# Layer 1 of a graph network on one core: the sums of s and t move from ScalarE to VectorE, with s in a PSUM bank

## The chip, the core and the metric

The kernel runs on one core of a Trainium2 chip: TensorE (PE in the profile; PEld is its weight load), VectorE (DVE), ScalarE (ACT), GpSimd (POOL) and SyncE (SP), which work side by side and wait for each other by semaphores. SBUF is the working memory; PSUM, 8 banks of 128 partitions x 512 fp32, is where TensorE writes. The metric is the time of one execution on the device in microseconds (us); less is better. Before the change the median of nine runs is 1860.69 us (1857.22 to 1868.44).

## What is computed

Two layers over 4096 nodes of 512 features, with one sparse 4096 x 4096 adjacency matrix, all in fp32. Layer 0 is a graph convolution. Layer 1, in which the change lies, is an attention layer. The reference, cut to it:

```
h = relu(layernorm(x))
s = (h @ W) @ a[:512]            # one number for each destination node i
t = (h @ W) @ a[512:]            # one number for each source node j
e = leaky_relu(s[i] + t[j], 0.2)
attention = softmax(where(adj > 0, e, -1e12), axis=1)
negative  = -softmax(where(adj > 0, -e, -1e12), axis=1)
x = x + elu(concat([attention @ h, negative @ h]) @ wtrans)
```

## The kernel before

**Layer 0** (the first 950 us or so) multiplies the dense adjacency and x, builds lists of neighbours, and writes to HBM eight tables with one row for each node: its 512 features, its t, and mask bytes. These tables are filled in part by copies from one to the next; the last ones (`copy_rows`, L498) are issued by SyncE while layer 1 runs.

**Layer 1** (`sparse_layer1`) goes through 62 blocks of 64 destination nodes, two to a pair; a pair is a tile of 128 nodes. (Two more blocks, those of `PAIR0` = 16, are done ahead of it.) The pairs come in the order 17, 20, 18, 19, 21, 22 and so on; k counts the blocks in that order from 0, so even k is the first block of a pair and odd k its second. Row r is the block's number (pair 19 has the blocks 38 and 39).

For each pair, GpSimd gathers rows of a table by index (`gather1`, L506) into three tiles g of 8, 7 and 7 chunks of 128 neighbours. One of the 22 chunks is the pair's own 128 rows, which SyncE loads plainly (`load_own`, L520) as the last chunk of the middle tile. The first block of a pair uses the first two tiles, its second block the last two; each block so has two parts, and the middle tile is the second part of the first block.

`weights(r)` makes the weights of a block, part by part. A part has n chunks (7 or 8) and 64 columns for each:

- z = s + t for each chunk: ScalarE, one instruction for each chunk (L1765), 128x64, with t as its bias. s is a row of the block's s, broadcast over the partitions, in SBUF.
- y = 0.2 z (ScalarE, L1767), z = max(z, y) (VectorE, L1768), e = exp(z) and z = exp(-z) (ScalarE, L1773).
- p = mask > 0 times e, and the same with z (VectorE, L1777, two for each part).

z and e are PSUM banks. After both parts, one reduction on VectorE (L1787, "total") adds the block's weights over its chunks.

`product(r)` has TensorE sum "total" over the partitions (cs, L580), multiply the weights and the gathered rows into u (L556, 40 or 44 matmuls of 128x512), and VectorE invert the sums (rl, L585 and L588); ScalarE scales u into us (L1815). `turn` transposes us (tp, L595; ScalarE copies it out, L602). `project1` multiplies by `wtrans` (o, L1826): its first half at odd k, its second in `finish1` at the next even k. `finish1` then takes the minimum with 0 (eo, L1843), exp (L1844), the maximum plus x1 (y, L1846) and the last sum (eo, L1847), and SyncE stores the tile (L1848). The load of x1 for a tile (L1838) and the store stand in SyncE's queue ahead of the next table copies and own load.

For each k the program is written in the order `product(r_k)`; table copies when k % 6 is 1; `gather1` two pairs ahead; `weights` of the block two places ahead; `turn` of the block before; the half of a projection. A scheduler sets each engine's own order from that; GpSimd's gathers and a few others are pinned to the written order. Every PSUM tile (z, e, cs, u, tp, o) is one bank from a pool of eight, handed out in the written order, and as the built program shows the bank chosen is the one whose last reader comes earliest. The first instruction that writes a bank waits for the last reader of the tile that held it before.

`RB` is 64, a block's columns; `ROW_T` is the column of t in a table row. `scores` (L524) is an older helper by which VectorE sums s and t of a whole part in one instruction; before the change only the blocks done ahead of the 62 use it, with s in SBUF.

## Time and profile before

One execution was profiled; it took 1864.22 us, of which the span of the instructions is 1862.4.

| what | value |
|---|---|
| median of nine runs | 1860.69 us |
| profiled execution, and its span | 1864.22 us, 1862.4 us |
| busy in the span: PE, DVE, ACT, POOL | 1835.8, 1274.3, 936.2, 826.0 us |
| L1765, ScalarE's sums by chunk | 899 instructions (s, s_first), about 320 ns each |
| L1768, L1777, VectorE, 128x448 or 128x512 | 0.62 to 0.70 us each |
| L1787, VectorE's reduction | 62, 3373 ns each |
| L506, GpSimd's gathers | 672, 956 ns each |
| 1200 to 1300 us: PE, DVE, ACT, POOL busy | 100.0, 55.9, 60.6, 75.0 us |
| 1500 to 1600 us: PE, DVE, ACT, POOL busy | 100.0, 67.2, 70.8, 75.4 us |

How to read the views: a line of groups or of a timeline names a source line, engine, operation, the tile written and those read (buffer numbers left out), and its time. "[1.94 <-DVE rl L585]" at its end is the idle time of that engine just before it, and whose event ended it by the profile; where several were waited for, the last is named, and an engine's event may be a neighbour of the one that mattered. Times of a timeline count from the start of the span. A lower TensorE clock shows as longer matmuls.

### The profile page before, as it was taken

How to read it: one execution, taken by the hardware profiler on the slowest of the kernel's cores; microseconds unless marked ns; L12 is line 12 of the kernel's file. 1: busy time of each engine (PE TensorE's matmuls, PEld its weight loads, DVE VectorE, ACT ScalarE, POOL GpSimd, SP SyncE). 2: the span in 40 equal slices, each digit the busy share in tenths (PEclk: the TensorE clock that was granted, in tenths of full speed). 3: DMA queues.
4: the chain of work that ended last, by engine and by line, in shares of the span. 5: the costliest groups of instructions: out<-in, count | busy, mean ns of one | idle time of the engine just before them, and what ended most of it. 6: DMA issues, size and time to landing. Idle time of an engine off the chain costs nothing.

```text
span 1862.4 us, 24509 instructions
## 1 busy us (share of the span) xinstructions
PE 1835.8 (99%) x7708; PEld 1040.0 (56%) x7708; DVE 1274.3 (68%) x2758; ACT 936.2 (50%) x2165; POOL 826.0 (44%) x919
## 2 busy tenths in 40 slices
PE   8999999999999999999999999999999999999998
PEld 3444448888888888888644333333333333333333
DVE  6766669798979998897344566565656567665661
ACT  6777763322222321222235576665766677666661
POOL 3101000012332122422167677777776777777740
PEclk9999999999999999999998999999999999999999
DMA  9999976849685859585899789999898999989860
GB/s 370 402 333 333 336 236 201 250 154 297 196 254 162 281 159 291 155 268 155 251 324 362 250 271 320 339 303 333 287 340 275 335 298 297 299 281 300 298 213 25
DMA packets 217219, 504.33 MB, mean 271 GB/s; under 512 B 35060, under 2 KB 69396, under 8 KB 217079
## 3 DMA queue, kind: packets, MB, share of 16 engines
q0 software_dynamic: 62560, 233.71, 37.9%
q1 hardware_dynamic: 114240, 236.49, 37.7%
q10 hardware_dynamic: 40278, 32.47, 5.7%
q8 instruction: 63, 1.03, 0.2%
q14 instruction: 78, 0.63, 0.1%
HBM read 457.77 MB, written 103.45 MB: 301 GB/s over the span
## 4 chain that ended last, share of the span: by engine, by line
PE 85%; DMA 6%; DVE 3%; ACT 3%; issue 2%; POOL 1%; ACTq 0%; DVEq 0%; SPq 0%
PE p L1105 33%; PE u L556 24%; PE o L1826 10%; PE acc L1064 5%; PE yp L890 5%; DMA g<-table 3%; PE q L1465 3%; DMA ar<-in_adj 2%; PE tp L595 1%; ACT z L1765 1%; DMA g<-table,idx 1%; PE counts L867 1%; POOL g L506 1%; PE tx L831 1%; PE cs L1541 1%
## 5 line engine op out<-in xcount | busy, mean ns | idle before, releaser
L506 POOL DMA_INDIRECT g<-table,idx x672 | 642.6, 956 | 290.3 <-issue 171.3
L556 PE MATMUL u<-g,p 128*64 128x512 f32 x2604 | 574.2, 596 | 0.0
L556 PEld LDWEIGHTS u<-g,p 128*64 128x64 f32 x2604 | 183.1, 137 | 339.2 <-issue 313.7
L442 POOL DMA_INDIRECT ld<-lst,off x160 | 144.3, 902 | 344.4 <-DMA ld<-lst,off 165.8
L1765 ACT ACTIVATE z<-s,g 128x64 f32<-128x64 f32 x812 | 259.8, 320 | 52.6 <-DMA g<-table 30.3
L1105 PE MATMUL p<-y,at 128*128 128x256 f32 x832 | 248.0, 380 | 0.0
L1105 PE MATMUL p<-y,sums 128*128 128x256 f32 x832 | 247.4, 379 | 0.0
L1105 PE MATMUL p<-t,sums 128*128 128x256 f32 x832 | 245.3, 379 | 0.0
L1826 PE MATMUL o<-wt,ut 128*128 128x512 f32 x496 | 228.1, 604 | 8.6 <-DVE rl L585 7.2
L1768 DVE TENSOR_TENSOR z<-z,y 128x512 f32<-128x512 f32 (+1 forms) x124 | 80.5, 649 | 213.8 <-ACT y L1767 211.4
L1787 DVE TENSOR_REDUCE total<-p 128x128 f32<-128x1920 f32 (+1 forms) x62 | 209.1, 3373 | 2.1
L1105 PEld LDWEIGHTS p<-t,sums 128*128 128x128 f32 x832 | 158.0, 190 | 21.7 <-issue 0.2
L1105 PEld LDWEIGHTS p<-y,at 128*128 128x128 f32 x832 | 157.1, 190 | 23.2 <-issue 2.2
L1105 PEld LDWEIGHTS p<-y,sums 128*128 128x128 f32 x832 | 158.0, 190 | 21.5
L1826 PEld LDWEIGHTS o<-wt,ut 128*128 128x128 f32 x496 | 91.1, 194 | 102.1 <-issue 92.0
L930 ACT ACTIVATE m<-at 128x1024 uint8<-128x1024 f32 x110 | 113.1, 1047 | 54.1 <-DVE prod L1020 15.3
L852 ACT ACTIVATE junk<-ar 128x1024 bf16<-128x1024 f32 x128 | 134.5, 1051 | 9.3 <-DMA ar<-in_adj 5.2
L1777 DVE SCALAR_TENSOR_TENSOR p<-g,e 128x512 f32<-128x512 uint8 (+1 forms) x124 | 79.1, 638 | 74.4 <-ACT e L1773 51.6
L1105 PE MATMUL p<-t,at 128*128 128x256 f32 x416 | 124.0, 380 | 1.2 <-DVE w L975 1.2
L1064 PE MATMUL acc<-y,at 128*128 128x512 f32 x256 | 120.2, 594 | 0.0
L890 PE MATMUL yp<-w_sb,hx_t 128*128 128x512 f32 x256 | 118.5, 606 | 0.4 <-DVE hx_t L836 0.4
L800 ACT ACTIVATE rrb<-rrb 128x1 f32<-128x1 f32 x32 | 6.5, 203 | 214.1 <-DVE rrb L799 209.8
(220 smaller groups left out, 2038.0 us busy)
## 6 DMA issues: line engine op xcount, KB each, us to landing
ar<-in_adj SPq DMA_DIRECT2D x128, 512.0 KB, 6.2
at<-in_adj_t SPq DMA_DIRECT2D x112, 512.0 KB, 5.3
table<-table SPq DMA_DIRECT2D x49, 1032.0 KB, 9.3
table<-m ACTq DMA_DIRECT2D x48, 256.0 KB, 8.0
g<-table,idx POOLq DMA_INDIRECT x672, 5.0
g<-table SPq DMA_DIRECT2D x32, 322.0 KB, 6.0
at<-in_adj_t SPq DMA_DIRECT2D x32, 256.0 KB, 7.0
xr<-in_x SPq DMA_DIRECT2D x32, 256.0 KB, 6.2
```

Of the source, the lines that this page charges most:

```text
L442: return nc.gpsimd.indirect_dma_start(out=lst_dram[g][e % TURNS][:, :], out_offset=bass.IndirectOffsetOnAxis(ap=off[g][:, e, c : c + 1], a ...
L506: i = nc.gpsimd.indirect_dma_start(out=gt[:, k, :], out_offset=None, in_=table[2 * n // RPT], in_offset=bass.IndirectOffsetOnAxis(ap=idx[n ...
L556: i = nc.tensor.matmul(u[h * RB : (h + 1) * RB], p[:, k, h].rearrange("p g i -> p (g i)"), row(k), start=begin and k == HALVES[r % 2][h][0 ...
L852: nc.scalar.activation(junk, ar, AF.Identity, accum_out=parts[j][:, c : c + 1])
L890: nc.tensor.matmul(yp, hx_t[j][:, c * P : (c + 1) * P], w0_sb[:, c, :], start=c == 0, stop=c == FC - 1,)
L930: nc.scalar.activation(m, at, AF.Sign)
L1064: nc.tensor.matmul(a, at[:, 0, it * P : (it + 1) * P], y0[j], start=j == 0, stop=j == NJ - 1)
L1105: i = nc.tensor.matmul(out, left[:, x * P : (x + 1) * P], right, start=jp == 0 and first, stop=jp == NP - 1 and (final or not first),)
L1765: nc.scalar.activation(z[:, c], s, AF.Identity, bias=t[:, c])
L1768: nc.vector.tensor_tensor(z, z, y, ALU.max)
L1787: nc.vector.tensor_reduce(total, q, AX.X, ALU.add)
L1826: i = nc.tensor.matmul(halves[j], uts[j][:, g, c, :], wts[g][:, c, :], start=g == 0 and c == 0, stop=g == 1 and c == FC - 1,)
```

## The change

- The pool of eight PSUM banks can be replaced in mid-program: `new_banks` closes it and opens others. After the step k = 6 it opens one bank of its own, "row", and a pool of seven for everything else.
- From then on (the blocks from the tenth of the order on, since `weights` runs two places ahead), ScalarE copies the row of s for four pairs (128x512) into that bank when a new row begins, seven times in all.
- `weights` then calls `scores` once for each part, with s read from that bank, in place of ScalarE's instruction for each chunk.
- The pools of PSUM wait by tile (`reuse_waits="tile"`), as those of SBUF did already.

```diff
-    ps = ctx.enter_context(tc.tile_pool(name="ps", bufs=8, space=PSUM))
+    psum = ctx.enter_context(ExitStack())
+    ps = {}
+
+    def new_banks(name, n, own=()):
+        psum.close()
+        for tag in (*own, "ps"):
+            bufs = n if tag == "ps" else 1
+            pool = tc.tile_pool(name=f"{name}{tag}", bufs=bufs, space=PSUM, reuse_waits="tile")
+            ps[tag] = psum.enter_context(pool)
+
+    new_banks("all", 8)
...
-                s = srow[r // 8][:, r % 8 * RB : (r % 8 + 1) * RB]
+                s = srow[r // 8]
+                if "row" in ps:
+                    if r // 8 not in s_bank:
+                        s_bank.clear()
+                        s_bank[r // 8] = ps["row"].tile(
+                            [P, 4 * P], F32, tag="row", name=f"s_bank{r // 8}"
+                        )
+                        nc.scalar.copy(s_bank[r // 8], s)
+                    s = s_bank[r // 8]
+                s = s[:, r % 8 * RB : (r % 8 + 1) * RB]
...
-                    for c in range(n):
-                        nc.scalar.activation(z[:, c], s, AF.Identity, bias=t[:, c])
+                    if "row" in ps:
+                        scores(s, z, t)
+                    else:
+                        for c in range(n):
+                            nc.scalar.activation(z[:, c], s, AF.Identity, bias=t[:, c])
...
+                if k == 6:
+                    new_banks("few", 7, ("row",))
```

The helper that is called, unchanged:

```
    def scores(s, z, t):
        n = z.shape[1]
        return nc.vector.tensor_tensor(
            z, t.to_broadcast([P, n, RB]), s.unsqueeze(1).to_broadcast([P, n, RB]), ALU.add
        )
```

More of the change, by code (lines that the diff above doesn't have):

```diff
@@ L328, in gcn_gat_kernel @@
     const = ctx.enter_context(sbuf(name="const", bufs=1))
-    ps = ctx.enter_context(tc.tile_pool(name="ps", bufs=8, space=PSUM))
+    psum = ctx.enter_context(ExitStack())
[7 more added lines that the diff above has]
+    new_banks("all", 8)
     dram = ctx.enter_context(tc.tile_pool(name="dram", bufs=1, space=DRAM))
     def bank(name):
-        return ps.tile([P, 512], F32, tag="ps", name=name)
+        return ps["ps"].tile([P, 512], F32, tag="ps", name=name)
     ones = const.tile([P, P], F32, name="ones")
@@ L591, in turn_u @@
     def turn_u(r, u, ut, pin=False):
-        tp = ps.tile([P, FC, 2, 2, SB], F32, tag="ps", name=f"tp{r}")
+        tp = ps["ps"].tile([P, FC, 2, 2, SB], F32, tag="ps", name=f"tp{r}")
         for c in range(FC):
@@ L712, in sum_counts @@
         def sum_counts(g):
-            o_ps = places[g] = ps.tile([NH, NE + 1, NK + 1], F32, tag="ps", name=f"o_ps{g}")
+            o_ps = places[g] = ps["ps"].tile([NH, NE + 1, NK + 1], F32, tag="ps", name=f"o_ps{g}")
             for e in range(NE + 1):
@@ L1878, in sparse_layer1 @@
             with_late = (2 * pairs[0], 2 * pairs[0] + 1)
-            lates, halves = {}, {}
+            lates, halves, s_bank = {}, {}, {}
             order = [r for n in pairs for r in (2 * n, 2 * n + 1)]
```

## The prediction

> **What bounds the kernel now.** I first read the page's busy shares: TensorE is busy for 99% of the span, at nearly full clock. Busy only says where to look, so the next view is the chain that ended last, and the third is what TensorE waited for in layer 1 (from 950 us on).

> ```profile
> PE 1835.8 (99%) x7708; PEld 1040.0 (56%) x7708; DVE 1274.3 (68%) x2758; ACT 936.2 (50%) x2165; POOL 826.0 (44%) x919
> PEclk9999999999999999999998999999999999999999
> PE 85%; DMA 6%; DVE 3%; ACT 3%; issue 2%; POOL 1%; ACTq 0%; DVEq 0%; SPq 0%
> ```

> ```profile
> PE o L1826 <- DVE rl L585: 7.2, 4, 2.6
> PE o L1826 <- DVE y L1846: 1.3, 1, 1.3
> PE o L1860 <- ACT ut L602: 0.5, 1, 0.5
> ```

> The second fence (us in total, times, longest) is the point: after 950 us TensorE stands still for 9.0 us in all. A pair of blocks costs it 26.6 us (44 products 9.6, turn and projection 4.1, sums 0.2, 40 products 8.7, the same again), end to end. So ScalarE work that goes away is worth nothing in itself; only those gaps can shrink, and the gap that a new wait makes is paid in full.

> Where are the gaps? The TensorE timeline shows them at 1026.3 (2.6 us) and 1058.9 (1.35), both before the first block that the change touches, then at 1300.9 (1.94), 1382.9 (2.2) and 1466.8 (0.46). The last three have one cause, here for 1300.9 (timelines of SyncE, ScalarE, VectorE, TensorE; start, us, instruction, idle before it):

> ```profile
> 1271.17 2.54 SPq L498 DMA_DIRECT2D table<-table  x3
> 1274.02 0.68 SPq L520 DMA_DIRECT2D g<-table  x1
> ...
> 1294.16 0.32 ACT L1765 ACTIVATE z<-s,g 128x64 f32<-128x64 f32 x1 [7.83 <-DMA g<-table]
> ...
> 1301.98 0.68 DVE L1846 SCALAR_TENSOR_TENSOR y<-o,x 128x512 f32<-128x512 f32 x1
> ...
> 1302.81 3.67 PE L1826 MATMUL o<-wt,ut 128*128 128x512 f32 x8 [1.94 <-DVE rl L585]
> ```

> Every sixth step (k = 13, 19, 25, 31) SyncE puts three table copies ahead of the load of the block's own rows; that load lands 22.5 to 23.0 us after the first copy is issued (an own load without copies ahead lands in 6.0). ScalarE's sum of that one chunk waits, VectorE's total and y come 8.4 us after the landing, and the next projection waits for y to free its bank. k = 13 passes: there y ends at 1220.07 and the projection starts at 1220.91. The 2.2 us gap also costs clock: the eight projections after it took 5.37 us, not 3.60.

> **The change, part by part.**

> 1) ScalarE. Blocks from the tenth of the order on (53 of 62) lose their chunk sums: 768 of the 899 of L1765, at 320 ns, are 246 us, and 7 copies into the bank (nearest row: 128x512 in 0.60) add 4. All of it lies beside TensorE: 0 us by itself. Between copies, totals come every 24.9 us when VectorE and ScalarE catch up (1298.0, 1322.9, 1347.8), so the weights' chain regains only 1.7 us per pair; with 9.3 us less ScalarE in a pair it becomes bound by the gathers instead.

> 2) VectorE gains 106 sums of a part. The trace shows none from PSUM. Nearest rows: L527, the same sum from SBUF, 621 and 693 ns; L1768, which reads and writes PSUM, 633 and 699. I take 0.65, ends 0.62 and 0.75; VectorE was 60% busy in this stage and gets 2.6 us more in 26.6, hidden. [...]

> 3) GpSimd must not be slowed: its 21 gathers of a pair at 0.95 us plus 0.30 issue take 26.3 of 26.6 us. L1768 and L1777 run among them with one operand in SBUF, and the gathers beside them stay at 0.95. The new sum has that form: 0.

> 4) Banks: 8 become 7 after k = 6. In the changed kernel as built, TensorE's order is unchanged but its waits are not. At k = 7 the sum of block 39 (cs) takes the bank of the projection o of node tile 20 and waits for that tile's y. Before, it took the bank of the sum before it. TensorE's and VectorE's rows there:

> ```profile
> 1100.12 3.60 PE L1826 MATMUL o<-wt,ut 128*128 128x512 f32 x8
> 1103.56 0.28 PE L580 MATMUL cs<-ones,total 128*128 128x1 f32 x2
> 1103.76 9.66 PE L556 MATMUL u<-g,p 128*64 128x512 f32 x44
> ```

> ```profile
> 1107.25 3.51 DVE L1787 TENSOR_REDUCE total<-p 128x128 f32<-128x1920 f32 x1
> 1110.67 0.68 DVE L1843 TENSOR_SCALAR eo<-o 128x512 f32<-128x512 f32 x1
> 1111.27 0.68 DVE L1846 SCALAR_TENSOR_TENSOR y<-o,x 128x512 f32<-128x512 f32 x1
> ```

> TensorE is ready at 1103.56; y ends at 1111.95, behind a 3.5 us reduction, and VectorE's order up to it is unchanged. All products and projections stand behind that cs: **+8.4 us**, once (ends 7 and 9.5, as ScalarE's chain in front of the reduction shifts). Then the clock: after the 2.6 us gap at 1026.3 eight projections took 6.56 us (3.0 lost), after 2.2 us 1.8 were lost, after 1.94 none. For 8.4 us I take **+2.5** (ends 0 and 3.4). [...]

> 5) The order on VectorE. In a pair's first block the sum of the second part now stands ahead of the two products p of the first part, and that sum waits for the own load. Before, those products ran while ScalarE waited. With 7 banks the sum and product of the block that TensorE is at wait for the banks which these two free. Price at k = 19, in the times of before: projection o ends at 1263.8, so y can end about 1265.5 (it was 1269.97, held back by ScalarE); rl, max and eo 1.4, issue 0.4: copies at 1267.3, own rows at 1290.0 (+22.7); sum 0.65, two products 1.25, 0.1 of signalling: 1292.0. TensorE wants the sum at 1290.42 and the product at 1290.62: **1.4 us**, at four places = 5.6. In return the old waits end: the y that caused them now comes 10.4 us after the landing, 1300.4, while the turn that needs it comes at 1300.2 + 1.4. So 1.94 + 2.2 + 1.8 of clock + 0.46 = **-6.4** go. Ends for the new waits: 0 (y so early that the rows land in time) and 2.7 us each with 1.8 of clock (y 1.2 later): 0 to 18.

> 6) SyncE: one 0.5 MB table copy moves ahead by a pair, and four loads of s ahead of an own load (0.8 us of issue; the own load lands 5 us before the gathers beside it: 1570.01 + 6.0 against 1576.6 + 4.8): 0, to +1.

> **Sum:** 8.4 + 2.5 + 5.6 - 6.4 + 1 (the chance of clock loss at the four places) = +11.1; I take **+11.5**. The profiled execution took 1864.22 us (span 1862.4 and 1.8 around it): 1875.7 by its own time. It stands 3.5 us above the median of the nine runs, 1860.69, and a median is wanted: **1872 us**.

> **The rivals.**

> A, faster. The bank wait at k = 7 is covered, because y of tile 20 comes before 1103.6, and the relieved ScalarE removes the three late gaps: -6.4 and new waits of at most 2, so 1856. For it: the gaps are ScalarE's and the copies' work. Against: y would have to come 8.4 us sooner, and nothing ahead of it on VectorE or ScalarE changes. It decides only if the wait costs under 2 us. 0.06.

> B, no change: the wait at k = 7 is half hidden (5 us with clock) and the four late places gain it back: 1861. 0.08.

> C, slower still: y comes 1 us later in the pairs before the copies, each of the four waits is 2.5 us, above the 2.2 that cost clock: 10.9 + 17 - 6.4 = +21.5, 1882. For it: 1.4 against 2.2 is a small distance, and the own load hangs on y through SyncE's order. 0.20.

> D, GpSimd becomes the bound: if each new sum held up a gather for 0.63 us, 4 in a pair make 2.5, less 0.3 of slack, over some 23 pairs, less 12 us by which totals run ahead of their products: 10.9 + 39, 1910. Against: part 3. 0.03.

> E, the change doesn't do what it says: ScalarE's L1765 stays. The built order shows 106 sums on VectorE, so 0.

> **How the numbers follow.** Forecast 0.63 (1866 to 1878), A 0.06, B 0.08, C 0.20, D 0.03. Least change that a measurement can tell is about 0.2%, 3.7 us. Slower: forecast, C, D and a little of B: 0.87; same: most of B, 0.07; faster: A, 0.06. The range reaches from the forecast's low end less what B adds to C's: 1864 to 1883; it leaves out A, D and part of B.

> **What would show it.** Right: TensorE idle for 7 to 9.5 us once, near 1103 us, released by VectorE's y, and half clock after it; no gap ahead of a projection at the copies' pairs, but one of 1 to 2.5 us ahead of a sum or product (cs or u), 10 us earlier; sums of L527 at 0.65 us; gathers at 0.95. Wrong: no gap near 1103; or gaps at the copies above 2.2 us with projections of 5 us after them (C); or gathers over 1.0 us (D).

## The result, and the profile after

The changed kernel takes 1873.42 us (median of ten runs, 1869.65 to 1878.46), the kernel before on the same chip 1861.58: 1.0064 times as long, 95% interval 1.005 to 1.0077. On another chip, with six runs, the two were 1869.24 and 1860.25, ratio 1.0046 (1.003 to 1.0062). So the change costs 9 to 12 us. The profiled execution took 1866.31 us (span 1864.4).

Two of the chips used below took 2001 and 2022 us for the kernel before, and in the profiles from there TensorE stands still inside products for 50 to 78 us for no reason that the profile names; the runs from there are told by their ratios, and no cause is drawn from their size.

First the engines' busy times in the profile after, then two kinds of groups with their shapes kept apart (count | busy us, mean ns | idle before).

```profile
PE 1832.0 (98%) x7708; PEld 1038.9 (56%) x7708; DVE 1325.6 (71%) x2864; ACT 710.6 (38%) x1404; POOL 826.1 (44%) x919
```

```profile
L537 DVE TENSOR_TENSOR z<-g,s_bank 128x448 f32<-128x448 f32 x80 | 49.9, 623 | 93.7 <-DMA g<-table,idx 91.1 <-issue 2.6
L537 DVE TENSOR_TENSOR z<-g,s_bank 128x512 f32<-128x512 f32 x26 | 18.0, 693 | 15.6 <-DMA g<-table,idx 15.5
...
L516 POOL DMA_INDIRECT g<-table,idx x672 | 640.6, 953 | 294.3 <-issue 169.2 <-DMA table<-m 56.7 <-PE u L566 39.5
```

The work went where the change puts it: ScalarE 226 us less, VectorE 51 more, the gathers untouched (956 ns before, 953 now). TensorE's busy time hardly moves, so the loss must be time in which it waits. These are its waits from 940 us on (us in total, times, longest), which the prediction showed for the kernel before:

```profile
PE cs L590 <- DVE y L1868: 8.2, 1, 8.2
PE cs L590 <- DVE p L1799: 2.6, 3, 1.3
PE o L1848 <- DVE rl L595: 2.6, 1, 2.6
PE o L1848 <- DVE y L1868: 1.4, 1, 1.4
PE u L566 <- DVE p L1799: 0.9, 4, 0.2
...
```

Lines 3 and 4 are the two early gaps that both kernels have (and the line left out is their 0.5 us at the very end). The late gaps ahead of a projection (1.94, 2.22 and 0.46 us before) are gone; in their place stands one wait of 8.2 us for y, and small ones of a sum (cs) or product (u) for p. The long one, TensorE and then VectorE (start, us, instruction, idle before it):

```profile
1093.88 3.60 PE L1848 MATMUL o<-wt,ut 128*128 128x512 f32 x8
1105.63 0.59 PE L590 MATMUL cs<-ones,total 128*128 128x1 f32 x2 [8.15 <-DVE y L1868]
1106.15 11.40 PE L566 MATMUL u<-g,p 128*64 128x512 f32 x44
```

```profile
1101.02 3.37 DVE L1809 TENSOR_REDUCE total<-p 128x128 f32<-128x1920 f32 x1
...
1104.90 0.68 DVE L1868 SCALAR_TENSOR_TENSOR y<-o,x 128x512 f32<-128x512 f32 x1
```

cs of block 39 is ready to go at 1097.48 and starts when y of tile 20 has been written, behind the reduction. The 44 products after it take 11.40 us in place of 9.66, and cs twice its time (0.59 in place of 0.28): half clock (granted clock 0.50 from 1102.86 to 1109.69).

A second profile of the changed kernel (taken as one of the experiments) has the same wait for y, 8.1 us, but more at the table copies. Its waits for p, then SyncE, VectorE and TensorE at k = 13:

```profile
...
PE cs L590 <- DVE p L1799: 5.5, 4, 2.0
...
```

```profile
1194.61 1.96 SPq L508 DMA_DIRECT2D table<-table  x3
1197.99 0.33 SPq L530 DMA_DIRECT2D g<-table  x1
...
1219.27 0.63 DVE L537 TENSOR_TENSOR z<-g,s_bank 128x448 f32<-128x448 f32 x1 [12.41 <-DMA g<-table,idx]
1219.81 0.68 DVE L1799 SCALAR_TENSOR_TENSOR p<-g,e 128x512 f32<-128x512 uint8 x1
...
1220.63 0.35 PE L590 MATMUL cs<-ones,total 128*128 128x1 f32 x2 [2.03 <-DVE p L1799]
```

VectorE stands still for 12.41 us at the sum of the second part, which starts 24.66 us after the first copy is issued; the product p of the *first* part (128x512), ready long before, stands behind that sum, and TensorE's next sum waits for the bank that this product frees. The profile names a gather as the releaser of the sum, and the landing of the own rows is not recorded at this place. At k = 19 of the same profile it is (the record of the own load, then VectorE's sum):

```profile
L530 SPq DMA_DIRECT2D g<-table x1: 326/326/326, 1280.6 to 1280.6; - x1
DMA to landing us min/median/max: 20.6/20.6/20.6
```

```profile
1301.33 0.63 DVE L537 TENSOR_TENSOR z<-g,s_bank 128x448 f32<-128x448 f32 x1 [12.18 <-DMA g<-table,idx]
```

Issued at 1280.61, the own rows landed at 1301.2, and the sum started 0.1 us later, though here, too, a gather is named. It is the same at k = 31 (1446.20 + 19.1 = 1465.3, and 1465.43), and in the first profile at k = 19 (1275.96 + 18.7 = 1294.7, and 1294.80). So the sum waits for the own rows, and the experiments with the own rows first test it.

### The profile page after: what moved, and what is told of

It reads as the page before. It is cut to its first block, busy times and chain, and to the rows that moved or that the text cites. A ratio compares the mean times of both kernels' runs of the same rounds, so it can differ in the third digit from the quotient of the medians.

```text
span 1864.4 us, 23447 instructions
## 1 busy us (share of the span) xinstructions
PE 1832.0 (98%) x7708; PEld 1038.9 (56%) x7708; DVE 1325.6 (71%) x2864; ACT 710.6 (38%) x1404; POOL 826.1 (44%) x919
## 4 chain that ended last, share of the span: by engine, by line
PE 85%; DMA 6%; DVE 5%; POOL 2%; issue 1%; ACT 1%; ACTq 0%; DVEq 0%; POOLq 0%; SPq 0%
PE p L1115 29%; PE u L566 27%; PE o L1848 10%; PE acc L1074 5%; PE yp L900 5%; DMA g<-table,idx 3%; PE q L1475 3%; DMA ar<-in_adj 2%; POOL g L516 2%; PE tp L605 2%; PE counts L877 1%; DVE key L439 1%; DVE lst L437 1%; DMA ld<-lst,off 1%; PE tx L841 1%
## 5 line engine op out<-in xcount | busy, mean ns | idle before, releaser
L1115 PEld LDWEIGHTS p<-y,sums 128*128 128x128 f32 x832 | 158.0, 190 | 21.5
L1789 ACT ACTIVATE y<-z 128x512 f32<-128x512 f32 (+1 forms) x124 | 69.2, 558 | 228.4 <-DVE z L537 227.8
L537 DVE TENSOR_TENSOR z<-g,s_bank 128x448 f32<-128x448 f32 (+1 forms) x106 | 67.9, 640 | 109.3 <-DMA g<-table,idx 106.6
L1795 ACT ACTIVATE e<-z 128x512 f32<-128x512 f32 (+1 forms) x124 | 67.1, 542 | 127.0 <-DVE z L1790 127.0
```

Source lines behind the costliest of these rows:

```text
L1115: i = nc.tensor.matmul(out, left[:, x * P : (x + 1) * P], right, start=jp == 0 and first, stop=jp == NP - 1 and (final or not first),)
L1789: nc.scalar.activation(y, z, AF.Copy, scale=ALPHA)
```

## The experiments

From each profile three things were read: the gaps and half clock at k = 7, those at the four copies' places (k = 13, 19, 25, 31), and the time from the start of the sum of step k = 6 to the last matmul, which leaves out what varies earlier. "Over before" is that time less 764.5 us, the same of the kernel before; the last column is the difference of the medians on one chip. A half clock's loss is the time of the products (or of the projection) over their usual time, 9.66 (or 3.67) us; at k = 7 the sum cs adds 0.3, which the column leaves out.

| kernel | k = 7: gap + clock | four places: gaps + clock | over before, profile | over before, medians |
|---|---|---|---|---|
| before | 0 | late projections 4.6 + 1.7 | 0 | 0 |
| changed, first profile | 8.15 + 1.75 | 3.5 + 0 | +8.0 | +11.8 |
| changed, second profile | 8.14 + 1.75 | 6.4 + 1.7 | +12.7 | +9.0 |
| another bank | 3.47 + 2.4 | 9.1 + 1.7 | +11.4 | +8.8 |
| own rows first | 8.14 + 1.5 | 0 | +3.1 | +4.1 |
| written order | 8.13 + 1.9 | 2.0 + 0 | +6.1 | +6.3 |
| sums alone | 0 | 5.1 + 1.7 | 0.0 | -3.6 |
| sums alone, own rows first | 0 | 0 | -7.1 | -7.3 |

**1. Banks alone.** Seven banks and the copied row, but the sums stay on ScalarE.

```diff
                         nc.scalar.copy(s_bank[r // 8], s)
-                    s = s_bank[r // 8]
...
-                    if "row" in ps:
+                    if False:
                         scores(s, z, t)
```

> Banks alone: seven banks and the row of s copied into the eighth from k = 6 on, as in the changed kernel, but the row in the bank is never read; ScalarE keeps its sums per chunk, from SBUF. My theory: the gap at k = 7 (8.2 us, the sum of block 39 waiting for y of tile 20) and some 2 us of half clock after it stay, and the three late gaps of the kernel before stay too, because ScalarE still waits for the own rows: before + 10, about 1872. Rival 1, the sums themselves cost the time (VectorE or GpSimd slowed): no more than 1 us above the kernel before, 1862. Rival 2, one bank less is felt in every pair: well above the changed kernel, more than 1880, with gaps in most pairs.

Ratio 1.0038 (1.002 to 1.0055), on the chip of 2001 us. TensorE's waits there:

```profile
PE u L566 <- issue: 56.0, 48, 8.6
...
PE cs L590 <- DVE y L1867: 5.5, 1, 5.5
```

The wait for y at k = 7 is there without one sum on VectorE: the bank makes it. (It is shorter than 8.2 us here, but TensorE, too, came late to it, held up at the projection just before.) The first line is what is wrong on that chip, so nothing can be said of the late gaps.

**2. Sums alone.** VectorE's sums, s in SBUF, eight banks.

```diff
...
-                    if "row" in ps:
+                    if order.index(r) > 8:
                         scores(s, z, t)
...
-                if k == 6:
-                    new_banks("few", 7, ("row",))
```

> Sums alone: VectorE forms the sums of a part from the tenth block of the order on, with s read from SBUF; all eight banks stay, no copy into a bank. My theory: no gap at k = 7, the late gaps of the kernel before (6.4 us with clock) go, new ones of 0 to 1 us at most at the four copies' pairs: 1855 to 1859. Rival 1, the sums cost the time: 1870 or more, with gathers above 0.95 us each (both operands now lie in SBUF) or VectorE's y later in every pair. Rival 2, nothing that moves off ScalarE matters: 1861.6, the late gaps unchanged.

On the chip of 2001 us the ratio was 1.0154 (1.0128 to 1.0181), with 74 us of waits inside products that the profile does not explain. On another chip:

> The same kernel as the sums alone of the first call (VectorE's sums from SBUF, eight banks, no copy). My theory: 1855 to 1859, no gap at k = 7, late gaps of the kernel before gone. Rival 1, from the first call's 1.015: the sums on VectorE cost something in every pair, 1885 or so, with gaps inside the products. Rival 2: 1861.6, nothing changes.

1857.71 against 1861.35, ratio 0.998 (0.9967 to 0.9992): **faster than before**. No gap at k = 7. TensorE's one new wait, and the groups to hold against those above:

```profile
PE u L566 <- DVE p L1791: 5.1, 4, 1.8
```

```profile
L537 DVE TENSOR_TENSOR z<-g,s 128x448 f32<-128x448 f32 x80 | 50.2, 628 | 112.2 <-DMA g<-table,idx 106.9 <-DMA g<-table 5.3
L537 DVE TENSOR_TENSOR z<-g,s 128x512 f32<-128x512 f32 x26 | 18.2, 699 | 37.3 <-DMA g<-table,idx 37.3
...
L516 POOL DMA_INDIRECT g<-table,idx x672 | 652.0, 970 | 279.4 <-issue 182.3 <-DMA table<-m 56.8 <-PE u L566 11.1
```

The sums cost TensorE nothing in a pair without copies, and at the copies the order on VectorE costs about as much with eight banks as with seven. The expectation of at most 1 us there was too low. Where the 3.6 us of the medians come from, the one profile does not show: from k = 6 on it is as long as that of the kernel before, 5.1 + 1.7 at the copies against 4.6 + 1.7. Experiment 7 shows what the sums gain once the copies' places are out of the way.

**3. Another bank for block 39.** One more tile is taken when the seven banks open; VectorE writes a column of it.

```diff
                     new_banks("few", 7, ("row",))
+                    nc.vector.memset(bank("skip")[:, :1], 0.0)
```

> The changed kernel with one tile more taken from the seven banks right after they are opened (VectorE writes one column of it, after y of tile 20), so that the sum of block 39 gets another bank and waits only for the turn before it. All else as in the changed kernel. My theory: the gap of 8.2 us at k = 7 and its 2 us of half clock go, the 3.5 us at the copies' pairs stay: changed kernel - 10.2, so 1863 if the medians' whole difference of 11.8 us lies elsewhere than in what the profile shows, 1859 if the profile's sum (8.2 + 2.05 + 3.5 - 6.4 = 7.3 over the kernel before) is all there is. Rival, the gap only moves to the next projection or turn, which waits for the same y: changed kernel - 2 or less, 1871 or more.

On the chip of 2001 us: ratio 1.0237 (1.0205 to 1.027). On another:

> The same kernel as the skipped bank of the first call, which ran on a chip where the kernel before, too, took 2001 us, 7.5% more than in the runs of before, with TensorE standing still in the middle of products for 1 to 2 us with nothing that the profile names; so this is the same question again. My theory: the gap of 8.2 us at k = 7 and its 2 us of half clock go: 1859 by the profile's sum, 1863 by the medians. Rival 1, the gap only moves to another instruction that waits for the same y: 1871 or more. Rival 2, from the first call's 1.024: the new order costs TensorE its instructions or its data in every pair, 1880 or more, with gaps inside the products.

1870.17 against 1861.35, ratio 1.0042 (1.0027 to 1.0057). My expectation of 1859 to 1863 fell. TensorE's waits:

```profile
...
PE cs L590 <- ACT ut L612: 3.5, 1, 3.5
...
```

The wait for y is gone, but the sum now has the bank of a turn and waits for ScalarE's copy of it (ut), 3.5 us; that still costs clock (the 44 products after it take 12.09 us in place of 9.66). And the four places happened to cost 9.1 us, with 1.7 of clock. (At k = 13 this profile names the own rows themselves: VectorE's sum there stands after 13.29 us, "<-DMA g<-table".) So it shows that the bank's holder sets the gap, and that "another bank" is not "no wait".

**4. The changed kernel with the own rows first, and the changed kernel again.** SyncE's own load is written ahead of the copies of its step, and every own load is held to the written order (not shown); the two ran on one chip.

```diff
-                if k % 6 == 1 and k // 6 < len(later_tables):
-                    for j, n in GROUPS[-3 if k > 12 else -2 :]:
-                        tc.keep_in_program_order(copy_rows(nc.sync, later_tables[k // 6], j, n))
                 if k + 4 - k % 2 < len(order):
                     for a in ((0,), (1, 2))[k % 2]:
                         gather1(order[k + 4 - k % 2] // 2, a)
+                if k % 6 == 1 and k // 6 < len(later_tables):
+                    for j, n in GROUPS[-3 if k > 12 else -2 :]:
+                        tc.keep_in_program_order(copy_rows(nc.sync, later_tables[k // 6], j, n))
```

> The changed kernel with SyncE's load of the own rows written ahead of the table copies of the same step; banks and sums as in the changed kernel. My theory: the gap of 8.2 us at k = 7 with its half clock stays; at the four copies' pairs the sum of the second part no longer waits for the own rows, and the gaps ahead of the sum of the next block go. In the one profile of the changed kernel those were 3.5 us in all, in the profile of the skipped bank 9.1 with 2 us of half clock after one of them: so the changed kernel - 3.5 (1870) if the first is typical, - 9 (1864) if the second is. Rival 1, the own rows are not what those places wait for: 1873, gaps unchanged. Rival 2, the copies, now later, let the gathers from the new table wait: 1875 or more.

> The changed kernel once more, for a second profile of it and its time on the same chip. In the first profile the gaps from k = 7 on explain 7.3 us over the kernel before, but the medians differ by 11.8. My theory: the difference is in the landing of the own rows at the four copies' pairs, which moves by a microsecond or two from execution to execution: the median is again 1872 to 1875, and this profile shows 8.2 us at k = 7 and between 3 and 10 us in all at the four places, each gap as long as the sum of the second part is late. Rival, something else in the changed kernel varies (stages before k = 6, gaps in other pairs): then the four places show 3.5 again and the rest of the difference stands elsewhere.

Own rows first: 1864.38 against 1860.25, ratio 1.0018 (1.0008 to 1.0029). Changed: 1869.24, ratio 1.0046. TensorE's waits with the own rows first, and VectorE's sum at k = 13:

```profile
PE cs L590 <- DVE y L1867: 8.1, 1, 8.1
PE o L1847 <- DVE rl L595: 2.6, 1, 2.6
PE o L1847 <- DVE y L1867: 1.4, 1, 1.4
PE o L1881 <- ACT ut L612: 0.5, 1, 0.5
```

```profile
1212.45 0.63 DVE L537 TENSOR_TENSOR z<-g,s_bank 128x448 f32<-128x448 f32 x1 [5.85 <-DMA g<-table,idx]
```

All waits at the copies are gone, and the sum starts 6.8 us earlier than in the second profile above, though GpSimd began that pair's gathers at the same 1188 us in both. That settles that the sum waited for the own rows. The median of the changed kernel, 1869.24, lies below the 1872 to 1875 that I had expected.

The second profile bears on the other question, why the first explained 8 of 12 us. Gap and landing go together: where the sum started 22.6, 23.7, 24.1, 24.7 and 25.5 us after the copies began (the second profile and that of experiment 3), the gap ahead of TensorE's next sum was 0.30, 1.38, 1.80, 2.03 and 2.90 us. TensorE reaches that sum 23.7 to 24.0 us after the copies began, and at all twelve places of the three profiles the gap is the start of VectorE's sum, plus 1.36 us for it and the first product, less TensorE's arrival, within 0.03 us (and none where that is below zero). The start of the sum, and so by this reading the landing, moves by 3.3 us from one place to another (22.2 to 25.5 us); the first profile was one with early landings. Whether the ten timed runs of the first chip had late ones cannot be seen, since they left no trace.

**5. The written order.** The changed kernel with VectorE's sums and products of each part pinned to the order of the program, so that the products of the first part go ahead of the sum of the second.

```diff
-                        scores(s, z, t)
+                        tc.keep_in_program_order(scores(s, z, t))
...
-                        nc.vector.scalar_tensor_tensor(
+                        i = nc.vector.scalar_tensor_tensor(
...
+                        if "row" in ps:
+                            tc.keep_in_program_order(i)
```

> The changed kernel with VectorE's sums and its two products of each part held to the order in which they are written, so that in a pair's first block the two products of the first part stand ahead of the sum of the second part. Banks, sums, loads and copies as in the changed kernel. My theory: the gaps at the four copies' pairs (3.5 and 6.4 us in the two profiles of the changed kernel) come only from these two products, which wait behind a sum whose own rows are late; held to the written order they go, with what clock they cost, and the 8.2 us at k = 7 stay: the same 1864 as with the own rows first (ratio 1.002). Rival 1, the order isn't what matters, the block after is late anyway because its second part is: 1869 to 1873, the same gaps or gaps ahead of products a little later. Rival 2, the written order costs VectorE in other pairs: 1870 or more, gaps in pairs without copies.

On the chip of 2022 us: ratio 1.0128 (1.0098 to 1.0158). On another:

> The changed kernel with VectorE's sums and products held to the written order, once more, since the chip of its first run took 2022 us for the kernel before. My theory: no gap at the four copies' pairs, the 8.2 us at k = 7 stays with 1.75 of half clock: 1864, ratio 1.002, as with the own rows first. Rival 1, the block after is late anyway: 1869 to 1873. Rival 2, the written order costs VectorE in other pairs: 1870 or more, with gaps in pairs without copies.

1867.57 against 1861.31, ratio 1.0034 (1.0022 to 1.0046). The waits of cs and u for p are gone from the profile; a new one stands in their place:

```profile
PE tp L605 <- DVE rl L595: 2.0, 2, 1.6
```

It stands at k = 25 and 31 (0.43 and 1.56 us): with the block's second part late by as much as ever, the reduction and y come late, and the turn that follows the block's products waits for them. So my theory holds for the first wait, and rival 1 for a part: the order hides the late rows at two places and moves the wait at the others.

**6. The kernel before with the own rows first.** The edit of experiment 4, in the kernel before.

> The kernel before, eight banks and ScalarE's sums, with SyncE's load of the block's own rows written ahead of the table copies of the same step (k = 13, 19, 25, 31). My theory: the own rows land 6 us after their issue, not 22.5, nothing on ScalarE is late, and the three late gaps with their clock loss (1.94 + 2.2 + 1.8 + 0.46 = 6.4 us) go: 1855. Rival 1, the load cannot be issued earlier because its slot is not free: the gaps stay, 1861.6. Rival 2, the copies, now later, hold up the gathers from the new table: a new gap at k = 15 or later, over 1862.

> The kernel before with SyncE's own rows ahead of the table copies, the same kernel as in the first call, whose chip was slow for every kernel. My theory: the three late gaps of the kernel before, with their half clock (6.4 us), go: 1854 to 1856, and TensorE has no gap after 1060 us but the last. Rival 1, the gaps stay because ScalarE is late for another reason: 1860. Rival 2, the copies, now later, hold up the gathers: over 1862.

Both runs fell on the chips of 2001 and 2022 us: ratios 1.0017 (0.9999 to 1.0035) and 1.0015 (0.9989 to 1.0041). Neither profile has a gap ahead of a projection at the copies, but with TensorE held up elsewhere that proves little. What this edit alone is worth on the other chips stays open.

**7. Sums alone with the own rows first.** Experiments 2 and 4 together.

> The sums alone (VectorE, s in SBUF, eight banks, no copy into a bank) with SyncE's own rows ahead of the table copies of the same step. My theory: the sums alone, at 1857.7, had left 5.1 us of gaps and 1.75 of half clock at the four copies' pairs; with the own rows early these go, and what is left of gaps after 1060 us is the last one of 0.46: 1857.7 - 6 = 1852, ratio 0.995, faster than both kernels. Rival 1, the gathers or VectorE are late once the own rows aren't: 1857. Rival 2, the copies, now later, hold up gathers from the new table: 1860 or more.

1854.06 against 1861.31, ratio 0.9956 (0.994 to 0.9972): the fastest version. All of TensorE's waits from 940 us on:

```profile
PE o L1839 <- DVE rl L595: 2.6, 1, 2.6
PE o L1839 <- DVE y L1859: 1.8, 1, 1.8
PE o L1873 <- ACT ut L612: 0.5, 1, 0.5
```

From k = 6 on only the last half microsecond is left. Against the changed kernel with the own rows first (+4.1 on its chip), this version, without the bank, lies 11.4 us lower by the medians and about 10 by the profiles: what the bank costs.

One thing no experiment has by itself: the PSUM pools that wait by tile, which every kernel but the one before has from its start. The time before the sum of k = 6 was 1084.2 to 1091.1 us in the seven profiles of the changed kernel and its variants on these chips (six of them under 1089) and 1090.7 in the one of the kernel before. With one profile of that, an effect of a few microseconds there can't be told from what varies anyway.

## Why the prediction was right, step by step

The forecast was 1872, +11.5 over before; the medians say +11.8 and +9.0. By its own time the profiled execution was forecast at 1875.7 and took 1866.3. Two thirds of that lie outside the change: before the sum of k = 6 it was 6.3 us ahead of the profile of before (1084.4 against 1090.7), where half clock lay on TensorE for 10.2 us between 985 and 1035, in place of 23.9. From k = 6 on it was 8.0 us over, not 11.5: its own rows landed early (3.5 us of waits in place of 5.6), the microsecond for half clock at the four places did not come, and the half clock at k = 7 was 0.5 us cheaper.

1. *ScalarE's sums, 0 by themselves:* right. 226 us less on ScalarE moved no pair without copies.
2. *VectorE's sums, 0.65 us and hidden:* right, 623 and 693 ns. From a PSUM row they are no slower than from SBUF (628 and 699 in experiment 2). Of my ends, 0.62 and 0.75, no run shows the upper one.
3. *Gathers not slowed:* right, 953 ns. With both operands in SBUF they took 970 and 965 (experiments 2 and 7): rival D in very small, and hidden.
4. *The bank at k = 7, +8.4 and +2.5 of clock:* right; 8.15, and 1.75 with 0.3 more at the sum cs. Of my ends for the clock, 0 and 3.4, no run shows the upper one: at k = 7 it cost 1.5 to 2.4 us in the profiles of the table that have a wait there. Experiment 1 has the wait without the sums, 2 the sums without the wait, and 3 shortens it by another holder.
5. *The order on VectorE, 1.4 us at four places:* right in mechanism, and mis-sized twice. I took one landing, 22.7 us after the copies began; the runs show 22.2 to 25.5 for the start of the sum. And by my working TensorE wanted its sum 23.1 us after the copies (1290.42 less 1267.3); it came 23.7 to 24.0 after. So a place cost 0.2 to 3.1 us, and all four 3.5 or 6.4 against 5.6: the two errors pull in opposite directions. Experiment 4 takes all of it away, 5 a part.
6. *The old waits, -6.4:* right, 4.6 + 1.7 and none left.
7. *Half clock at the places, +1 for the chance of it:* 0 in one profile, 1.7 in the other.
8. *SyncE, 0 to +1:* nothing seen.

So the sum is 9.9 + 3.5 - 6.3 = +7.1 by the first profile and 9.9 + 8.1 - 6.3 = +11.7 by the second. The profiles themselves have +8.0 and +12.7; of the microsecond that is left, 0.3 is the sum cs at half clock, and the rest was not traced. That the forecast of +11.5 came within a microsecond of the first chip's +11.8 is in part luck: the landings alone move the four places by more than that, and the second chip's median is 2.5 us lower.

Rivals A and B needed y of tile 20 earlier; nothing moved it. C's half clock occurred, but not with a later y, which was its reason. The likeliest case came true. Of the later expectations on the chips other than those two four missed: the other bank, because I did not look up who reads that bank last; the places of the sums alone and of the written order, which I put too low; and the second median of the changed kernel, which I put too high.

## What to carry to other kernels

Where TensorE is the bound, price a change by the waits that it makes and ends, not by the work that it moves: here 226 us of ScalarE's work were worth nothing, and one tile's bank cost 10. When a pool is reopened or made smaller, list for the first tiles after it who held the bank and when its last reader runs. And an instruction that covers a whole part waits for the latest chunk of it, and holds all that stands behind it on its engine (here VectorE stood still for 12.41 us at one sum; with that chunk loaded first the idle time there was 5.85 us, and the kernel took 1864.38 us in place of 1869.24): load that chunk first.

## What else the runs showed of the hardware

```profile
1219.22:1222.63 3.41, 1.84 (x10) 0.93 (x12) 2.71 (x5) 1.45 (x4) 2.54 (x3) 1.00 0.90 310
1222.63:1226.04 3.41, 3.41 (x20) 1.13 (x16) 3.38 (x3) 1.18 (x4) 1.24 (x2) 1.00 0.87 268
1301.14:1304.55 3.41, 1.61 (x8) 0.87 (x10) 2.63 (x5) 1.37 (x3) 2.55 (x3) 1.00 0.96 338
1304.55:1307.96 3.41, 3.41 (x10) 1.19 (x8) 3.38 (x3) 1.26 (x4) 1.89 (x2) 0.50 0.78 257
```

The longer gap (2.03 us) lies across two windows and costs nothing; the shorter (1.80) lies almost wholly in one and halves the next. Other windows at full clock on the grid of their profile, from 1045 us on, with what TensorE was busy for: half clock followed after 0.00 us (changed, first profile, k = 7), 1.22 (before, k = 25), 1.57 (sums alone with the own rows first, 1056.51 us), 1.58 (sums alone, k = 19) and 1.65 (another bank, k = 13), and none after 1.45 (changed, first profile, 1096.03 us), 1.58 (before, k = 19), 1.64 (another bank, k = 19), 2.04 (changed, first profile, 1051.66 us), 2.06 (before, 1058.63 us) and 2.19 (another bank, k = 25). So in these rows it followed all at 1.22 us or less and none at 1.84 or more; between 1.45 and 1.65 us the busy time in the profile, whose matmul ends are modelled, doesn't tell the two kinds apart, and what does was not shown. Whether a gap of about 2 us cost clock depended on where it fell.

**Two chips were different.** On those where the kernel before took 2001 and 2022 us, the kernels with ScalarE's sums came within 1.0015 to 1.0038 of it, those with VectorE's sums at 1.0128 to 1.0237, though on the other chips these stood at 0.998 to 1.0042. The profiles there show TensorE idle for 50 to 78 us in products with no releaser. Why, and why the order of the kernels changes with it, was not tried.
